# An edge-gated graph layer on one core: edge sums for two tiles at a time, additions in place, one more place for fetched rows

## The chip, the cores and the metric

The kernel runs on one core of a Trainium2 chip. The metric is the device time of the program in microseconds, as the median of several runs. The kernel before takes 1149.22 us (three runs, 1148.77 to 1149.63). The profile is of one execution, recorded by the hardware profiler.

## The reference: a gated sum over neighbours

The input `x` has 16 batches of 1024 nodes with 256 features, the adjacency matrix `adj` is 1024x1024 and mostly zero (one entry in about 128, and the diagonal). Cut to what matters:

```python
pre_u = jnp.einsum('bud,dk->buk', h_t, W1[:d])
pre_v = jnp.einsum('bvd,dk->bvk', h_t, W1[d:])
hidden = jax.nn.relu(pre_u[:, :, None, :] + pre_v[:, None, :, :] + b1)
S = jax.nn.sigmoid(jnp.einsum('buvk,ko->buvo', hidden, W2)[..., 0] + b2[0])
a_t = jnp.einsum('buv,bud->bvd', S * A_a, h_t)
m_t = jnp.einsum('uv,bud->bvd', A_m, h_t) * h_t
z_t = beta1 * h_t + beta2 * (jnp.einsum('bvd,de->bve', a_t, Wa) + ba) + beta3 * (jnp.einsum('bvd,de->bve', m_t, Wm) + bm)
```

Both adjacency arguments are `adj`. For each pair of a source u and a target v that `adj` connects, and for each batch, a gate is computed from a row of 256 sums. The features of u then go into two sums at v: one weighted by the entry of `adj`, one by entry times gate. Two 256x256 products, biases and the input itself make the output.

## The kernel before

**Tiling.** Only the connected pairs are computed. Targets come in 8 blocks of 128 (`vt`), batches in 4 groups of 4 (`g`, `GB` = 4). A pair of group and target block is a block `k`, 32 in all, in the list `order`. The edges of a target block are put into slots: two windows of 64 targets, five tiles of 128 edge slots each, so that a block has ten tiles and the whole program 320 (`n` counts them, `s` is the tile within its block). `lists` works out, for each target block, which source each slot holds and its entry of `adj`. It is a generator, cut into pieces that are laid between other work: four lists are made ahead of the first tile, four in the course of the first 120 tiles.

**The table.** For each group a table in DRAM has one row of 8 KB per source: the 4x256 values of `pre_u` and the 4x256 features. `rows` (L434) computes the first half of it with products on PE (L427), a copy on ACT (L443) and a DMA write on SP (L446); `copy_h` copies the second half from the input. `halves` (L452) computes `pre_v` + b1 for the targets of the next block, as two parts that add up exactly, `X`; its subtraction on DVE is L463.

**A tile.** These functions make one tile:
- `fetch` (L493): an indirect DMA, issued by POOL, brings the 128 rows of a tile into one of `NF` = 6 places `fetched` (L496). Tile n uses place n modulo 6.
- `expand` (L564): two products on PE (L569) spread `pre_v` of the targets over the edge slots, into the PSUM tile `pc`, of which there are two.
- `left_adj` (L573): ACT writes the adjacency weights of the slots, once for each of the four batches, into `left` (L579).
- `gate` (L598): DVE adds `fetched` and `pc` into the single buffer `t` (L601, 128x1024). Four operations then take the relu times W2 and its sum, a batch each (L606, 128x256). ACT turns the four sums into gates (L609) and multiplies the weights by them (L612, four operations). Pieces of a list go between the L606 (`fill`).
- `aggregate` (L614): PE sums over the slots (L623): for each batch a product with 32 columns of weights, 16 targets by two kinds. The four batches lie side by side in the array. A tile has one or two such rows of four products, by the quarters of the window that its slots can belong to; each fp32 product shows as two instructions in the trace.

**The end of a block.** `half_end` (L628) copies finished sums from PSUM (L631, ACT), `turn_over` (L633) transposes them on PE (L641), copies them into `LT` (L644, ACT) and multiplies the plain sums by the features of the target (L654, DVE). `block_end` (L659) forms the products with Wa and Wm on top of the bias (L672), two batches at a time; ACT copies them to `z` (L675), DVE adds beta1 times the input (L676), and SP stores the result (L678). The input rows `h_blk` are loaded by SP (L775). All small products share two PSUM banks (`small`). The last block has an end of its own, `tail`.

**Order.** The order of instructions on each engine is that of the program, written out by hand as one loop over n (L745). A step n issues, in this order: the edge sums of tile n-1 and the fetch of the tile that takes its place; the gate of tile n; the adjacency weights of n+1; what is due (`do`, work put off by `after` to a later step); the products `expand` of n+2; and then the small products, by the value of s: transposes at s = 1, 7 and 9, block end at 3 to 6, `halves` at 0, 2, 3, 5 and 6. Rows of the table come at steps written out as numbers (`plan`, L732 to L737), of which the second pair, for groups 2 and 3, matters here: up to one per block at s = 8 and one at s = 1.

## Time and profile before

| | |
|---|---|
| median of three runs | 1149.22 us |
| span of the profiled execution, first to last instruction | 1165.8 us |
| time of the profiled execution apart from its span | the page gives none |
| mean granted TensorE clock | 0.976 (0.94 from 71 to 300 us, then 1.00) |
| PE, DVE, ACT, POOL busy | 94%, 91%, 77%, 38% of the span |
| additions L601 | 320, the first at 71.6 us, the last at 1145.4 us |
| fetched rows (POOL's DMA queue) | 300.5 of 391.4 MB |

The profiled span is 16.6 us above the median of the runs; sums are made against it and then scaled. Busy times are sums of the lengths of instructions, without overlap. PE is shown busy while a matmul is in its pipeline, so a full row of PE can still have room; PEld is its weight load. "Idle before, releaser" is the time that an engine stood before an instruction, and what ended it. A loop step takes (1145.4 - 71.6)/319 = 3.37 us on the mean.

### The profile page before, as it was taken

The page shows a single profiled execution, that of the slowest core. Times are in us where ns is not written, and L with a number is a line of the kernel's source. Part 1 is how long each engine was busy: PE and PEld are TensorE (multiplying, and loading weights), DVE is VectorE, ACT ScalarE, POOL GpSimd, SP SyncE. Part 2 cuts the span into 40 slices and gives each one's busy share as a digit, 9 for nine tenths or more (in the row PEclk, how much of TensorE's full clock was granted, in tenths as well). Part 3 has the DMA queues.
Part 4 walks back from the last instruction along what each step waited for, and adds up shares of the span by engine and source line. Part 5 has one row for each costly group of instructions (what it writes and reads, how often), then busy time and mean ns, then how long its engine had stood idle before and what let it go on. Part 6 is the DMA issues. An engine that isn't in the chain of part 4 may idle for free. (4 is left out here: it accounts for less than half of the span.)

```text
span 1165.8 us, 23918 instructions
## 1 busy us (share of the span) xinstructions
PE 1092.1 (94%) x7633; PEld 723.1 (62%) x7633; DVE 1056.2 (91%) x3487; ACT 893.5 (77%) x2624; POOL 439.9 (38%) x428
## 2 busy tenths in 40 slices
PE   7867899999999999999999999999999999999986
PEld 6744666666666666666666666666666666666553
DVE  7688889888999989999999999999999999999994
ACT  2346587767887878888888888888888888888873
POOL 1556645253335333443333333333333333333330
PEclk9868899999999999999999999999999999999999
DMA  9986898999999999999999999999998998999991
GB/s 286 298 307 223 277 372 312 362 320 331 342 320 323 396 379 336 358 350 402 389 374 369 355 364 356 360 364 383 371 375 324 361 322 333 334 339 328 328 346 60
DMA packets 147048, 391.40 MB, mean 336 GB/s; under 512 B 16753, under 2 KB 105329, under 8 KB 110705
## 3 DMA queue, kind: packets, MB, share of 16 engines
q0 software_dynamic: 50016, 300.50, 68.9%
q1 hardware_dynamic: 81616, 74.99, 20.0%
q10 hardware_dynamic: 15280, 14.29, 3.7%
q8 instruction: 63, 1.03, 0.3%
q14 instruction: 73, 0.59, 0.1%
HBM read 393.78 MB, written 50.33 MB: 381 GB/s over the span
## 5 line engine op out<-in xcount | busy, mean ns | idle before, releaser
L496 POOL DMA_INDIRECT fetched<-table,uidx x320 | 341.5, 1067 | 628.3 <-PE acc L623 447.2
L606 DVE SCALAR_TENSOR_TENSOR t<-t,w_b 128x256 f32<-128x256 f32 x1280 | 478.3, 421 | 19.3 <-ACT left L612 0.5
L601 DVE TENSOR_TENSOR t<-fetched,pc 128x1024 f32<-128x1024 f32 x320 | 389.3, 1217 | 41.4 <-PE pc L569 13.9
L623 PE MATMUL acc<-fetched,left 128*32 128x256 f32 x4096 | 336.2, 391 | 31.9 <-ACT left L612 26.2
L612 ACT ACTIVATE left<-left,gt 128x32 f32<-128x32 f32 (+1 forms) x1280 | 299.3, 304 | 10.4
L569 PE MATMUL pc<-X,mark 128*128 128x512 f32 x640 | 237.6, 453 | 6.2 <-ACT mark L562 5.0
L623 PEld LDWEIGHTS acc<-fetched,left 128*32 128x32 f32 x4096 | 130.6, 109 | 179.3 <-issue 52.4
L569 PEld LDWEIGHTS pc<-X,mark 128*128 128x128 f32 x640 | 97.2, 191 | 140.0 <-issue 89.3
L609 ACT ACTIVATE gt<-sc,b_b 128x4 f32<-128x4 f32 x320 | 96.2, 301 | 43.4 <-DVE t L606 40.8
L672 PE MATMUL misc<-w_m,LT 128*128 128x256 f32 x496 | 117.2, 379 | 0.0
L672 PE MATMUL misc<-w_a,LT 128*128 128x256 f32 x496 | 117.1, 379 | 0.0
L579 ACT ACTIVATE left<-onehot,val 128x128 f32<-128x128 bf16 (+1 forms) x320 | 116.5, 364 | 0.0
L427 PE MATMUL misc<-w_v,hT 128*128 128x256 f32 x448 | 107.3, 383 | 0.0
L427 PE MATMUL misc<-w_u,hT 128*128 128x256 f32 x416 | 101.2, 390 | 5.7 <-ACT few L329 3.6
L606 DVE DVE_READ_ACCUMULATOR t<-t,w_b 128x1 f32 x1280 | 104.0, 81 | 0.0
L672 PEld LDWEIGHTS misc<-w_a,LT 128*128 128x128 f32 x496 | 93.9, 189 | 15.1
L672 PEld LDWEIGHTS misc<-w_m,LT 128*128 128x128 f32 x496 | 93.8, 189 | 14.9
L382 POOL DMA_INDIRECT val<-in_adjT_dram,vidx x80 | 85.7, 1071 | 35.1 <-issue 22.4
L427 PEld LDWEIGHTS misc<-w_v,hT 128*128 128x128 f32 x448 | 86.0, 192 | 13.9
L427 PEld LDWEIGHTS misc<-w_u,hT 128*128 128x128 f32 x416 | 79.5, 195 | 17.3 <-ACT few L329 3.7
L631 ACT COPY ev<-acc 128x512 f32<-128x512 f32 x128 | 75.5, 590 | 14.6 <-PE acc L623 4.2
L675 ACT COPY z<-misc 128x512 f32<-128x512 f32 x62 | 36.3, 586 | 58.1 <-PE misc L672 38.8
(164 smaller groups left out, 947.9 us busy)
## 6 DMA issues: line engine op xcount, KB each, us to landing
h_blk<-in_x_dram SPq DMA_DIRECT2D x31, 512.0 KB
out_dram<-z SPq DMA_DIRECT2D x31, 512.0 KB
hT<-in_xT_dram SPq DMA_DIRECT2D x28, 512.0 KB
table<-in_x_dram ACTq DMA_DIRECT2D x24, 512.0 KB
table<-tab SPq DMA_DIRECT2D x24, 512.0 KB
fetched<-table,uidx POOLq DMA_INDIRECT x320
table<-in_x_dram SPq DMA_DIRECT2D x8, 512.0 KB
table<-fetched SPq DMA_DIRECT2D x8, 512.0 KB
```

What stands on the lines that cost most here:

```text
L382: nc.gpsimd.indirect_dma_start(out=val[:, i, j:j + 1], out_offset=None, in_=adj_flat, in_offset=bass.IndirectOffsetOnAxis(ap=vidx[:, i, j: ...
L427: nc.tensor.matmul(p[:, bb * D:(bb + 1) * D], hT[:, 2 * h + bb, i, :], wt[:, i, :], start=(i == 0 and not begun), stop=(i == DC - 1), skip ...
L496: nc.gpsimd.indirect_dma_start(out=fetched[n % NF], out_offset=None, in_=table[g], in_offset=bass.IndirectOffsetOnAxis(ap=uidx[:, vt * NW ...
L569: nc.tensor.matmul(pcs[n][:, c], marks[n // TW][:, j * P:(j + 1) * P], cuts[k][:, w, c], start=True, stop=True)
L579: nc.scalar.activation(lefts[n][:, :m, :, 0, :], onehot[:, i, o:o + m, :].unsqueeze(2).to_broadcast([P, m, GB, V]), AF.Copy, scale=val[:, ...
L601: nc.vector.tensor_tensor(t, fetched[n % NF][:, :GD].rearrange("p (b d) -> p b d", b=GB), pcs.pop(n).rearrange("p (b d) -> p b d", b=GB), ...
L606: nc.vector.scalar_tensor_tensor(t[:, b, :], t[:, b, :], 0.0, w2_b, ALU.max, ALU.mult, accum_out=sc[:, b:b + 1])
L609: nc.scalar.activation(gt, sc, AF.Sigmoid, bias=b2_b)
L612: nc.scalar.activation(lefts[n][:, :m, b, 1, :], lefts[n][:, :m, b, 0, :], AF.Copy, scale=gt[:, b:b + 1])
L623: nc.tensor.matmul(accs[h][b * 2 * V:(b + 1) * 2 * V, r, :], left[:, i, b].rearrange("p k v -> p (k v)"), f[:, GD + b * D:GD + (b + 1) * D ...
L631: nc.scalar.copy(evs[q], accs.pop(q))
L672: nc.tensor.matmul(pz[:, bb * D:(bb + 1) * D], LTs[k][:, c, 2 * h + bb, i, :], wt[:, c, :], start=False, stop=(i == 0 and c == DC - 1), sk ...
```

## The change

Seven things change.
- The addition is a function of its own, `add`. It writes into the place of the fetched rows, and step n adds tile n+1 ahead of the gate of n. The gate works in place on the fetched rows; `t` is gone.
- Every second step (odd n) issues the edge sums of two tiles, n-3 and n-2, back to back, and then the two fetches that take their places; in the last three steps the sums follow at once.
- A place is taken from a list of free ones. There are 7, and after step 110 an eighth, in the memory of a new pool `lst`, which holds all buffers of the lists and is closed there.
- `left` has the adjacency weights twice instead of four times: its seven columns of 16 are laid out so that neighbouring batches share one. `LT` gets another order of its parts to match.
- `block_end` has no `z` and no copy on ACT: DVE reads the products from PSUM, adds and writes into `h_blk`, which is stored from there.
- The small products are moved: block end from s = 3 to 6 to s = 4 to 7, the transposes to s = 0, 2 and 8. Up to n = 120 they and `expand` stand ahead of addition and gate in the step, later behind.
- The last planned load of `plan` and its two row products come two steps earlier.

```diff
+    lst = ExitStack()
+    lists_done = lst.close
+    lst = lst.enter_context(tc.tile_pool(name="lst", bufs=1))
...
-    NF = 6
+    NF = 7
+    at_slot, free = {}, list(range(NF))
...
-        R = wk.tile([P, RC], FP, name="R", bufs=4)
+        R = lst.tile([P, RC], FP, name="R", bufs=4)
...
+        at_slot[n] = free.pop(0)
         nc.gpsimd.indirect_dma_start(
-            out=fetched[n % NF], out_offset=None, in_=table[g],
+            out=fetched[at_slot[n]], out_offset=None, in_=table[g],
...
-        lefts[n] = wk.tile([P, 2, GB, 2, V], FP, name="left")
-        nc.scalar.activation(lefts[n][:, :m, :, 0, :], onehot[:, i, o:o + m, :].unsqueeze(2).to_broadcast([P, m, GB, V]),
+        lefts[n] = wk.tile([P, 2, 2 * GB - 1, V], FP, name="left", bufs=5)
+        nc.scalar.activation(lefts[n][:, :m, 1::GB, :],
+                             onehot[:, i, o:o + m, :].unsqueeze(2).to_broadcast([P, m, GB // 2, V]),
                              AF.Copy, scale=val[:, i, j:j + 1])
...
+    def add(n):
+        t = fetched[at_slot[n]][:, :GD]
+        nc.vector.tensor_tensor(t, t, pcs.pop(n), ALU.add)
+
     def gate(n):
-        k, g, vt, w, j = where(n)
-        t = one.tile([P, GB, D], FP, name="t")
-        nc.vector.tensor_tensor(t, fetched[n % NF][:, :GD].rearrange("p (b d) -> p b d", b=GB),
-                                pcs.pop(n).rearrange("p (b d) -> p b d", b=GB), ALU.add)
+        m = len(QUARTERS[n % TW])
+        t = fetched[at_slot[n]][:, :GD].rearrange("p (b d) -> p b d", b=GB)
...
-            nc.scalar.activation(lefts[n][:, :m, b, 1, :], lefts[n][:, :m, b, 0, :], AF.Copy, scale=gt[:, b:b + 1])
+            nc.scalar.activation(lefts[n][:, :m, 2 * b, :], lefts[n][:, :m, 1 + b // 2 * GB, :],
+                                 AF.Copy, scale=gt[:, b:b + 1])
...
-                                 left[:, i, b].rearrange("p k v -> p (k v)"), f[:, GD + b * D:GD + (b + 1) * D],
+                                 left[:, i, 2 * b - b % 2:2 * b - b % 2 + 2].rearrange("p k v -> p (k v)"), f[:, GD + b * D:GD + (b + 1) * D],
...
-            LTs[k] = one.tile([P, DC, GB, 2, P], FP, name="LT")
+            LTs[k] = one.tile([P, GB, 2, DC, P], FP, name="LT")
...
-        after(step + (1 if k == BS - 1 else 2), times_h)
+        after(step + (1 if k == BS - 1 or w else 2), times_h)
...
-            nc.scalar.copy(z[:, sl], pz.rearrange("p (b d) -> p b d", b=2))
-            after(step + 2, lambda sl=sl: nc.vector.scalar_tensor_tensor(z[:, sl], hb[:, sl], be1, z[:, sl],
-                                                                         ALU.mult, ALU.add))
-        after(step + 3, lambda: nc.sync.dma_start(
-            out[g * GB:(g + 1) * GB, vt * P:(vt + 1) * P, :].rearrange("b p d -> p b d"), z))
+            after(step + 1, lambda sl=sl, pz=pz: nc.vector.scalar_tensor_tensor(
+                hb[:, sl], hb[:, sl], be1, pz.rearrange("p (b d) -> p b d", b=2), ALU.mult, ALU.add))
+        after(step + 2, lambda: nc.sync.dma_start(
+            out[g * GB:(g + 1) * GB, vt * P:(vt + 1) * P, :].rearrange("b p d -> p b d"), hb))
...
-                                                                             for i in range(2, NT - 1)), (223, 231, 233)))
+                                                                             for i in range(2, NT - 1)), (221, 229, 231)))
...
-        if 1 <= n <= total:
-            aggregate(n - 1)
-            fetch_val(2)
-            if n - 1 + NF < total:
-                fetch(n - 1 + NF)
-            if n % TW in (0, MID + 1):
-                half_end(n - 1, 0 if n % TW else 1)
+    def products(n, k, s):
+        nonlocal end, parts, piece, last
+        if (s == 2 and 0 < k < BS) or n == total:
             turn_over(k - 1, 1, 1, n)
-        if s in (3, 4, 5, 6) and 0 < k < BS:
-            if s == 3:
+        if s in (4, 5, 6, 7) and 0 < k < BS:
+            if s == 4:
                 end = block_end(k - 1)
                 next(end)
             go(end, n)
-        if s == 7 and k < BS:
+        if s == (8 if n < total - T else 7) and k < BS:
             turn_over(k, 0, 0, n)
             turn_over(k, 0, 1, n)
-        if s == 9 and k < BS:
-            turn_over(k, 1, 0, n)
+        if (s == 0 and 0 < k < BS) or n == total - 1:
+            turn_over(k - (s == 0), 1, 0, n)
...
+    add(0)
+    def refill():
+        nonlocal ahead
+        while free and ahead < total:
+            fetch(ahead)
+            ahead += 1
+    def gather_in(n):
+        aggregate(n)
+        free.append(at_slot.pop(n))
+        fetch_val(2)
+        refill()
+        if (n + 1) % TW in (0, MID + 1):
+            half_end(n, 0 if (n + 1) % TW else 1)
+    for n in range(total + 2):
+        k, s = divmod(n, T)
+        if n < total - 3:
+            last_in = n - 1 if n % 2 else done
+        else:
+            last_in = n
+        while done < min(last_in, total):
+            gather_in(done)
+            done += 1
...
+        if n < 120:
+            if n + 2 < total:
+                expand(n + 2)
+            products(n, k, s)
+        if n + 1 < total:
+            add(n + 1)
         if n < total:
             gate(n)
             if n + 1 < total:
                 left_adj(n + 1)
...
+        if n >= 120 and n + 2 < total:
+            expand(n + 2)
...
         fill(n, False)
+        if n >= 120:
+            products(n, k, s)
+        if n == ROOM:
+            lists_done()
+            more = main.enter_context(tc.tile_pool(name="more", bufs=1))
+            for i in range(MORE):
+                free.append(len(fetched))
+                fetched.append(more.tile([P, 2 * GD], FP, name=f"fetched{len(fetched)}"))
+            refill()
```

## The prediction

> **What bounds the kernel now.** I read the shares by engine first, then the stages, then single steps. PE is busy 94% and DVE 91% of the span, so the shares leave both open. The stages are in the table of busy time by stretch (columns: stretch, length, then busy time and count of each engine, TensorE clock, DMA share, GB/s); the two 10 us rows are from a finer one:

> ```profile
> 71.00:300.00 229.00, 208.46 (x1354) 138.50 (x1353) 196.47 (x670) 161.07 (x469) 114.34 (x112) 0.94 0.89 311
> 300.00:500.00 200.00, 194.40 (x1393) 128.50 (x1392) 190.71 (x646) 162.16 (x480) 81.92 (x77) 1.00 0.96 353
> 500.00:900.00 400.00, 395.96 (x2859) 260.83 (x2860) 378.13 (x1190) 338.71 (x1009) 138.88 (x129) 1.00 0.99 366
> 900.00:1146.70 246.70, 236.26 (x1704) 149.56 (x1704) 236.50 (x745) 203.63 (x619) 78.98 (x76) 1.00 0.90 327
> ```

> The same table for the line of the additions (L601) counts 58, 59, 125 and 79 tiles in them. A block is ten tiles, so a block takes 39.5, 33.9, 32.0 and 31.2 us. To see what a block is made of I went to the timeline of DVE (start, length) in a late block:

> ```profile
> 1107.41 0.74 DVE L676 SCALAR_TENSOR_TENSOR z<-h_blk,be,z 128x512 f32<-128x512 f32 x1
> 1108.08 1.21 DVE L601 TENSOR_TENSOR t<-fetched,pc 128x1024 f32<-128x1024 f32 x1
> 1109.32 0.42 DVE L606 SCALAR_TENSOR_TENSOR t<-t,w_b 128x256 f32<-128x256 f32 x1
> ...
> 1110.36 0.42 DVE L606 SCALAR_TENSOR_TENSOR t<-t,w_b 128x256 f32<-128x256 f32 x1
> ...
> 1110.88 1.22 DVE L601 TENSOR_TENSOR t<-fetched,pc 128x1024 f32<-128x1024 f32 x1
> 1112.21 0.43 DVE L606 SCALAR_TENSOR_TENSOR t<-t,w_b 128x256 f32<-128x256 f32 x1
> ```

> From start to start: L606 to the next L606 0.347; the last L606 to L601 0.52; L601 to L606 1.33, or 1.24 when another operation came before L601. With three 0.347 per tile and the five extra operations of a block (two L676 at 0.67, two L654 at 0.61, one L463 at 1.14), a block sums to 5x1.33 + 5x1.24 + 30x0.347 + 5x0.52 + 5x0.347 + 3.70 = 31.3 us. The measured period from one L676 (981.89) to the same one of the next block (1013.18) is 31.29. So DVE alone sets the late pace: from 900 on it waits 1.1 us in total. PE is "busy" because matmuls overlap in its records, and waits there for ACT. In 500 to 900 DVE's waits are 8.8 us, and DMA stands at a share of 0.99, with a ceiling near 1.03 where it is fullest (530 to 570: 1.02 to 1.05).

> PE pays at each change between the edge sums (32 columns) and full matmuls. Weight loads in the timeline of PE:

> ```profile
> 603.54 0.59 PEld L623 LDWEIGHTS acc<-fetched,left 128*32 128x32 f32 x16 [0.33 <-ACT mark L562]
> 604.54 0.30 PEld L569 LDWEIGHTS pc<-X,mark 128*128 128x128 f32 x2 [0.41 <-issue]
> ```

> Both loads stand idle at the change, 0.33 and 0.41, each tile. In matmul starts: 1.82 from eight L672 to L623 instead of 8x0.213 (0.11 lost), 1.00 for 16 L623 instead of four groups of 0.215 (0.14), 0.57 for two L569 instead of 0.43 (0.14): 0.39 us a tile.

> [...] independent operations start before the end of the one before (0.347 apart at a length of 0.42), and one that waits for its own engine starts 0.17 later. [...] L713 reads PSUM at 128x512 in 0.75, L676 SBUF in 0.75. [...] No row shows a landing.

> **The change, part by part.**

> *Additions in place, a tile ahead.* L601 no longer writes the single buffer t, so it stops waiting for the L606 just before it, and the first L606 finds its sum a tile old. In the built program the addition has lost its wait on DVE. Without a wait, a 128x1024 addition is followed after 1.14 (L463 at 1006.52, L601 at 1007.66), and an L606 after 0.347. Saved a block: 5x(1.33-1.14) + 5x(1.24-1.14) + 5x(0.52-0.347) = 2.3 us; new sum 29.0. From below: 0, if the gaps are fixed; from above 2.3. I take 2.3, since the list of waits of the built program shows the cause gone. It is work on the bounding engine.

> *Edge sums of two tiles together.* 160 pairs of changes fewer, 62 us of PE. PE isn't the bound, so this is worth nothing by itself: it is hidden behind DVE, and without that cover would be up to 1.9 us a block. Late, PE's own work (128 L623 in groups of four 6.9, 20 L569 4.3, 48 of L672 and L427 10.2, their 4 bias rows 0.9, 16 L641 1.7, changes 3.9) is 27.9, then 25.9. The sums move one to two tiles later, with them their fetches on POOL and the copies of acc on ACT: PE no longer meets a gate of the tile just done, which removes most of 26.2 us of PE waiting for L612.

> *Slots.* A row place is now held from the addition until the second of two sums. Before: a fetch issued at 614.41 served the addition at 628.98, a lead of 14.6. With seven places the sums of a pair can start when ACT has weighted the second tile, some 2 us into a DVE step (L609 0.30, L612 0.96, waits); with 1 us for the first sum and 1.07 for the issue (L496) its fetch is under way after about 4.5, and is wanted four steps after the start of that one: at 3.0 to 3.4 us a step 7.5 to 9 us ahead. The second has a step more, less its own 1 us of issue. From tile 110 on, an eighth place adds a step. [...] Upper: if landing takes the whole old lead, some 5 us for each of 55 pairs. The queue moves a fetch's share (77% of bytes) in about 3.0 us at 405 GB/s, so two ahead and itself make 9: just in time. I take a third of the gain before tile 110 as lost.

> *Output straight from PSUM.* 62 copies L675 (0.586 each, 0.48 start to start: 30 us) leave ACT, whose 58 us of waiting before them goes too; L683 then takes DVE as long as L676. New wait: the second product's bank is free only after L683 at the end of DVE's step 8. In the built program the second group of transposes of step 8 waits for it from tile 120 on. Behind it on PE stand, where there is a table row product (tiles 128, 138, 158, 188 to 228: 8 blocks), 8x0.213, then the edge sums of step 9 and the two L569 products of the tile that DVE adds at the start of step 10: 0.43 + 1.71 + 0.11 + 1.72 + 0.14 + 0.57 + some 0.2 of pipeline = 4.9 against a DVE step of 1.14 + 4x0.347 = 2.53. DVE loses 2.3 us in such a block, and 0.6 in one without the row product. PE then has nothing else to run in front.

> *The rest.* L579 writes half as much: by its two forms (386 ns at 128, 332 at 64) 54 ns less x192 and an estimated 27 x128, 14 us of ACT, hidden, as ACT is at 85%. The load of h_blk waits for the store to land, since both use one buffer: on SP the hT load and table write stand behind; two 0.52 MB transfers against six steps (18 us) until L683, hidden; uncovered, some 3 us a block. Moved transposes, pool renaming and the changed layout of LT keep counts and sizes: 0. The last tiles are summed at once, so the end is unchanged, and one more initial fetch costs POOL 1 us ahead of work that waits for lists: 0.

> **Sum against the profiled span.** Late, 7.9 blocks: (2.3-0.6)x7.9 = 13.4. 500 to 900, 12.5 blocks: DVE gives 2.3 less the mean wait (8x2.3 + 4.5x0.6)/12.5 = 1.7, so 0.6; DMA's floor 32.0x0.99/1.03 = 30.8 allows 1.2; the new wait will overlap some of the old 0.7, so I take 0.9: 11. 300 to 500: two thirds of 2.3, 5.9 blocks: 9. The first 229 us, where PE and DVE both fall short of full: the same 1.5, 5.8 blocks: 9. Together 42: span 1165.8 to 1124. The median of the runs is 1149.2, 0.986 of the span, and the page gives the execution no other time; scaled, 1149.2 - 42 = 1107.

> **The rivals.**
> *More of it arrives.* The new bank wait is absorbed, because PE, freed of changes and of ACT, runs further ahead. For: 25.9 of PE work in 29. Against: DMA's floor, 1.2 to 1.8 a block at a ceiling of 1.03 to 1.05. Late 2.3x7.9 = 18, middle 1.45x12.5 = 18, earlier 12 and 12: 1149 - 60 = 1089.
> *The gaps stay.* If 1.33 and 0.52 don't come from the own wait, or the bank wait costs every block 2.3, only the early relief of PE and ACT is left, some 6 us: 1143. Against: the 1.14.
> *Fetches late, slower.* With seven places, DVE waits at the addition for the first fetch of a pair. 42 us over 55 pairs is 0.76, so it decides when landings overrun the lead by 0.76 us on the mean, that is, take longer than about 9 us; at an overrun of 1 us it is 55 less 42, so 1162. For: share 0.96 and 0.99, two issued together. Against: the DVE waited only 2.8 us for fetches before, and the stages before tile 110 are the slowest, which lengthens the lead.
> *It comes out even,* where these meet.

> **How the numbers follow.** Forecast (1095 to 1126) 0.58, more of it 0.13, gaps stay 0.14, even 0.04, slower 0.11. Within 0.2%, 2.3 us, a measurement can't tell it from no change. Faster 0.85, same 0.04, slower 0.11. The range leaves out the slower tenth and the best half of the second case: 1084 to 1145; the forecast's own is 1095 to 1126.

> **What would show it.** L606 after the addition starts at 1.14, and the addition at 0.35 after L606; a late block at 29.0 to 29.8 between L683s; idle time before the weight loads of the edge sums once in two tiles; PE waiting for DVE's L683 at the transposes of step 8, and DVE right after for the products. Wrong, if DVE's waits name fetches by more than 30 us, or if the period late stays above 31.

## The result: slower, 1194 us instead of 1107

The changed kernel takes 1194.41 us (median of four runs, 1191.46 to 1196.33), the kernel before 1149.11 beside it: a ratio of 1.0392, 95% interval 1.0363 to 1.0421. The forecast was 1107 with a range of 1084 to 1145. The profiled execution took 1195.8 us with a span of 1193.9.

The table of busy time by stretch of the changed kernel, cut where tiles 0, 60, 120, 240 and 319 are added (columns: stretch, length, busy time and count of PE, PEld, DVE, ACT and POOL, TensorE clock, DMA share, GB/s):

```profile
71.80:298.70 226.90, 199.09 (x1380) 137.68 (x1383) 197.58 (x698) 158.20 (x474) 115.45 (x111) 0.94 0.92 325
298.70:515.30 216.60, 193.47 (x1413) 134.42 (x1405) 189.35 (x650) 156.50 (x479) 88.16 (x82) 0.95 0.92 331
515.30:926.90 411.60, 373.47 (x2764) 261.43 (x2764) 348.17 (x1143) 305.96 (x946) 124.92 (x121) 0.97 0.94 347
926.90:1168.30 241.40, 218.44 (x1713) 147.00 (x1714) 227.02 (x749) 188.78 (x601) 84.17 (x76) 0.96 0.92 334
```

In the kernel before, the same stretches took 237.8, 203.8, 384.4 and 247.8 us. By these two traces 10.9 us are won up to tile 60 and 6.4 from tile 240 on, and 12.8 and 27.2 are lost between. They must be read with care: the profiled execution of the kernel before has a span 16.6 us above the median of its runs here, so the two spans are 28 us apart and the medians 45. Some 17 us of the loss are in no comparison with this trace; the second group shows where to look for them. DVE is no longer full in the middle: 348 of 412 us, and the clock, which was 1.00 from 300 us on, is 0.95 to 0.97.

The gain that the prediction counted on is in the timeline of DVE (start, length), in a late block:

```profile
1104.31 1.21 DVE L606 TENSOR_TENSOR fetched<-fetched,pc 128x1024 f32<-128x1024 f32 x1
1105.44 0.42 DVE L614 SCALAR_TENSOR_TENSOR fetched<-fetched,w_b 128x256 f32<-128x256 f32 x1
...
1106.47 0.42 DVE L614 SCALAR_TENSOR_TENSOR fetched<-fetched,w_b 128x256 f32<-128x256 f32 x1
1106.82 1.22 DVE L606 TENSOR_TENSOR fetched<-fetched,pc 128x1024 f32<-128x1024 f32 x1
```

Addition to gate is 1.13 instead of 1.33, gate to addition 0.35 instead of 0.52. What took it back is in the list of waits (engine, line, waited for: us in total, times, longest). DVE and PE in the changed kernel:

```profile
DVE fetched L606 <- PE pc L574: 112.0, 51, 6.3
DVE fetched L606 <- DMA fetched<-table,uidx: 22.3, 20, 3.5
...
PE misc L649 <- DVE h_blk L683: 40.6, 20, 2.3
```

and the same line of DVE in the kernel before:

```profile
DVE t L601 <- PE pc L569: 13.9, 18, 2.0
```

From tile 120's addition to the end the sum of the two traces closes: DVE waits 78 us for products and rows where it waited 7 (the additions' two main lines, both traces cut at that tile), less 20 blocks at 2.3 us that its operations give back (46), is 25 more; measured are 678.6 less 652.6, 26. So the question is why the addition now waits for L574. The prediction had one reason at hand, the bank of L683, and it is there, exactly 20 times. In the timelines of PE and DVE of a block with a row product:

```profile
788.93 0.63 PE L649 MATMUL misc<-ident,ev 128*128 128x128 f32 x4 [1.90 <-DVE h_blk L683]
790.18 3.41 PE L431 MATMUL misc<-w_u,hT 128*128 128x256 f32 x8 [0.62 <-ACT LT L652]
793.52 1.93 PE L631 MATMUL acc<-fetched,left 128*32 128x256 f32 x32
795.38 1.19 PE L574 MATMUL pc<-X,mark 128*128 128x512 f32 x4
```

```profile
796.15 1.22 DVE L606 TENSOR_TENSOR fetched<-fetched,pc 128x1024 f32<-128x1024 f32 x1 [4.85 <-PE pc L574]
```

The chain is the one described (transposes, row product, two tiles' sums, products, addition), but DVE loses 4.85 us, not 2.3: the row product takes 3.41 us where eight such products took 1.89 in the kernel before, and the trace has TensorE at half clock from 789.7 to 793.1 us. Adding up the stretches that the trace records at half clock gives 126.5 us, 82.1 of it after 230 us; in the kernel before 57.5 and 6.3.

### The profile page after: what moved, and what is told of

The parts are those of the page before. It is cut to its first block, busy times and chain, and to the rows that moved or that the text cites. A ratio compares the mean times of both kernels' runs of the same rounds, so it can differ in the third digit from the quotient of the medians.

```text
span 1193.9 us, 23757 instructions
## 1 busy us (share of the span) xinstructions
PE 1047.5 (88%) x7633; PEld 730.3 (61%) x7633; DVE 1020.6 (85%) x3487; ACT 841.7 (70%) x2562; POOL 439.3 (37%) x428
## 3 DMA queue, kind: packets, MB, share of 16 engines
q8 instruction: 62, 1.02, 0.3%
## 4 chain that ended last, share of the span: by engine, by line
DVE 36%; PE 31%; issue 12%; ACT 10%; DMA 8%; POOL 1%; ACTq 0%; DVEq 0%; POOLq 0%
DVE fetched L614 17%; PE misc L431 10%; DVE fetched L606 10%; PE acc L631 10%; DMA fetched<-table,uidx 7%; PE pc L574 4%; ACT left L619 3%; PE misc L680 3%; PE misc L649 2%; DVE h_blk L683 2%; ACT LT L652 2%; DVE low L467 2%; ACT gt L617 1%; PE misc L435 1%; DVE LT L663 1%
## 5 line engine op out<-in xcount | busy, mean ns | idle before, releaser
L606 DVE TENSOR_TENSOR fetched<-fetched,pc 128x1024 f32<-128x1024 f32 x320 | 388.4, 1214 | 135.7 <-PE pc L574 112.0
L614 DVE SCALAR_TENSOR_TENSOR fetched<-fetched,w_b 128x256 f32<-128x256 f32 x1280 | 474.5, 417 | 0.0
L631 PE MATMUL acc<-fetched,left 128*32 128x256 f32 x4096 | 272.7, 400 | 2.6 <-ACT left L619 2.6
L574 PE MATMUL pc<-X,mark 128*128 128x512 f32 x640 | 222.9, 448 | 15.7 <-DVE fetched L606 7.3
L574 PEld LDWEIGHTS pc<-X,mark 128*128 128x128 f32 x640 | 107.3, 190 | 98.8 <-issue 44.4
L649 PE MATMUL misc<-ident,ev 128*128 128x128 f32 x512 | 83.2, 287 | 67.4 <-DVE h_blk L683 40.6
L431 PE MATMUL misc<-w_u,hT 128*128 128x256 f32 x416 | 117.4, 435 | 15.9 <-ACT LT L652 8.8
L649 PEld LDWEIGHTS misc<-ident,ev 128*128 128x128 f32 x512 | 62.2, 145 | 92.4 <-ACT gt L617 43.7
L584 ACT ACTIVATE left<-onehot,val 128x64 f32<-128x64 bf16 (+1 forms) x320 | 102.8, 321 | 0.0
L614 DVE DVE_READ_ACCUMULATOR fetched<-fetched,w_b 128x1 f32 x1280 | 102.1, 80 | 0.0
```

The lines of the kernel that those rows point to most:

```text
L431: nc.tensor.matmul(p[:, bb * D:(bb + 1) * D], hT[:, 2 * h + bb, i, :], wt[:, i, :], start=(i == 0 and not begun), stop=(i == DC - 1), skip ...
L574: nc.tensor.matmul(pcs[n][:, c], marks[n // TW][:, j * P:(j + 1) * P], cuts[k][:, w, c], start=True, stop=True)
L584: nc.scalar.activation(lefts[n][:, :m, 1::GB, :], onehot[:, i, o:o + m, :].unsqueeze(2).to_broadcast([P, m, GB // 2, V]), AF.Copy, scale=v ...
L606: nc.vector.tensor_tensor(t, t, pcs.pop(n), ALU.add)
L614: nc.vector.scalar_tensor_tensor(t[:, b, :], t[:, b, :], 0.0, w2_b, ALU.max, ALU.mult, accum_out=sc[:, b:b + 1])
L631: nc.tensor.matmul(accs[h][b * 2 * V:(b + 1) * 2 * V, r, :], left[:, i, 2 * b - b % 2:2 * b - b % 2 + 2].rearrange("p k v -> p (k v)"), f[ ...
```

## The experiments

Two theories to begin with. **Bank:** the wait for L683's bank is the cause, only dearer than thought. **Clock:** PE, with less to do and in bursts of two tiles, leaves stretches idle and is then halved. A third came up after the second group. The runs fell on chips on which the kernel before takes 1149 (the changed kernel, the second and fifth group) or 1169 to 1173 us (the other groups), so each ratio is to the kernel before in the same group; the changed kernel as it is ran on the first kind alone. The one trace of the kernel before has a span as on the second kind (1165.8 us, where the runs there have 1162 to 1177 and those on the first kind 1142 to 1155), though its chip is not known. "From tile 120" is from that tile's addition to the end of the profiled execution.

**First group: without the bank wait, and with more work on PE.** The first issues what is due (`do`, L683 among it) between addition and gate:

```diff
+        if n >= 120:
+            do(n)
         if n < total:
             gate(n)
...
-        do(n)
+        if n < 120:
+            do(n)
```

> From tile 120 on, the work that is due is done between the addition and the gate of a step, so DVE frees the bank of the second product about 1.4 us sooner in step 8; nothing else moves. Theory A (PE stands for that bank in step 8, 20 times 2.0 us, its clock is halved after such a stand, and DVE then waits for the products of expand): the stand falls from 1.9 to about 0.5 us, the halved stretches after tile 120 mostly go, DVE's wait for expand after tile 120 falls from 78 us to under 35, time about 1150 (1140 to 1165). Theory B (the two sums together, or seven places, make PE and the fetches late, the bank is a bystander): within 10 us of 1194.

The second moves the second transposes and the row product to step 9 (the planned load of the last block goes two steps back with it):

```diff
-            turn_over(k, 0, 1, n)
+            if not 120 <= n < total - T:
+                turn_over(k, 0, 1, n)
+        if s == 9 and 120 <= n < total - T:
+            turn_over(k, 0, 1, n)
...
-            at.update((n, k) for n in pieces)
+            at.update((n + (n >= 120 and n % T == 8), k) for n in pieces)
```

> From tile 120 on, the second group of transposes and the row product of step 8 go to step 9, behind the edge sums and the expand products; the last planned row products are back at 231 and 233. PE then meets the bank a step later, when it is long free. Theory A: no wait of PE for L683 left, block period 29 to 31 us after tile 120, time 1135 to 1155. Theory B: within 10 us of 1194.

The third has ACT copy the output from its bank to a used part of LT at once, and DVE read it there:

```diff
+            z = LTs[k][:, 2 * h].rearrange("p k c n -> p (k c n)")
+            nc.scalar.copy(z, pz)
```

> One part undone: ACT copies the output product out of PSUM again (into a used part of LT), which frees the bank at once, and DVE adds from SBUF. Theory A: no wait of PE for L683, though ACT gets 62 copies (30 us) back and stands for PE before them; time 1140 to 1165. Theory B: no change, or slower by up to 10 us through ACT.

The fourth leaves the wait and gives PE two useless products ahead of the first transposes of step 8:

```diff
+        if w == 0 and q == 0 and 120 <= step < total - T:
+            for i in range(WARM):
+                nc.tensor.matmul(pt.rearrange("p r k c v -> p (r k c v)"), w_a[:, 0, :P], w_a.rearrange("p c k -> p (c k)"), start=True, stop=True)
```

> As the changed kernel, with two extra 128x512 products (about 1.7 us of PE, their output is overwritten) ahead of the first transposes of step 8 from tile 120 to 310: PE works where it stood, the bank comes no sooner. This tells the wait itself from the halved clock. If the halved clock after the stand does much of the harm: the halved stretches after tile 120 go and the time falls by 15 to 30 us, to 1165 to 1180. If the wait alone does it: 1190 to 1215, as the extra products cost nothing while PE waits and something where it doesn't.

| edit | ratio (95%) | from tile 120 | at half clock |
|---|---|---|---|
| L683 sooner | 1.0622 (1.0544 to 1.07) | 684.6 | 125.8 |
| transposes apart | 1.055 (1.0456 to 1.0644) | 672.8 | 137.0 |
| copy by ACT | 1.0636 (1.0541 to 1.0731) | 681.9 | 160.9 |
| two useless products | 1.0309 (1.0256 to 1.0362) | 661.9 | 92.1 |

None of the three without the bank wait is clearly better than the changed kernel: 672.8 from tile 120 at best, where two profiles of that kernel, on the faster chips, have 678.6 and 672.0. The waits of DVE from tile 120 on when the transposes are apart:

```profile
DVE fetched L606 <- PE pc L574: 42.5, 20, 9.1
DVE fetched L606 <- PE acc L631: 17.0, 14, 1.8
```

The bank theory falls. The wait for L683 is nearly gone (0.9 us with the transposes apart, 6.0 with L683 sooner, 40.6 in the changed kernel), and the additions still wait for PE, by the two lines 59.5 us where the changed kernel has 78 and 71; what is saved there comes back as other waits of DVE, and the stretch is as long as it was. With L683 sooner, DVE waits 29.9 us at L663 for ACT instead. The clock theory gains: the run with useless work is the best of the four, and from tile 120 on no block has a stretch at half clock (clock 1.00 from 979.1 to 1038.7 us, two late blocks, where the changed kernel has 0.97 from 956.6 to 1017.7). But it is still slower than the kernel before, and from tile 120 on its DVE waits 40.8 us for products and 18.6 more by the line of the edge sums.

**Second group: one part alone, one part undone.** The changed kernel again; the kernel before with nothing but the addition in place and a tile ahead; the changed kernel with sums of one tile a step; the changed kernel with the addition back at its own gate.

> The changed kernel unaltered, next to the three below on one chip. If the early blocks (tiles 10 to 120) were 30 us longer in the first four experiments because of their edits, this run shows its old start, tile 120 at 515 us, and about 1194. If they were longer because of the chip, tile 120 starts near 545 here too, and the kernel before is again some 20 us above its 1149.

```diff
+    def add(n):
+        t = fetched[n % NF][:, :GD]
+        nc.vector.tensor_tensor(t, t, pcs.pop(n), ALU.add)
...
+        if n + 1 < total:
+            add(n + 1)
         if n < total:
             gate(n)
```

> The kernel before with one part of the change alone: additions in place, a tile ahead. Edge sums stay single, the output still goes through a copy, six places. Clock theory (what hurts is that TensorE gets idle lumps and is then halved for 3.4 us): TensorE keeps its 27.9 us of work in small groups, hardly any stretch at half clock after 250 us, late block 29 to 30, 20 to 40 us below the kernel before on the same chip. Rival, the addition ahead is itself what hurts (a place is held a step longer, the fetch has a step less): VectorE waits for fetched rows by more than 30 us and the time is that of before or above.

```diff
-            last_in = n - 1 if n % 2 else done
+            last_in = n - 1
```

> The changed kernel with the pairing alone undone: the edge sums of one tile in every step, all else as changed. Clock theory: time at half clock falls from 126 us to 60 to 80, since the bursts and lumps of two tiles are gone; 25 to 45 us below the changed kernel on the same chip, with TensorE's wait for L683 in step 8 still there. Rival, the bank wait or the order from tile 120 on is the cause whatever the sums do: within 10 us of the changed kernel. Rival, TensorE becomes the bound with its 62 us back: late block above 31.

```diff
-        if n + 1 < total:
-            add(n + 1)
         if n < total:
+            add(n)
             gate(n)
```

> The changed kernel with the addition put back to the step that uses it (still in place), pairing and the rest as changed. VectorE's late step is long again, 31.3 a block. Clock theory: TensorE, with less work and a longer step, is idle more and is halved at least as often as in the changed kernel, 110 us or more, and the time is equal to the changed kernel's or up to 25 us above. Rival, the addition ahead is what hurts: the time comes back to within 10 us of the kernel before.

| kernel | ratio (95%) | DVE's wait for products | lead, tiles 120 to 239 / 240 to 309 |
|---|---|---|---|
| before | 1 | 13.9 | 1.1 / 2.7 |
| changed, again | 1.0463 (1.0418 to 1.0507) | 111.2 | 1.5 / 1.9 |
| before, addition ahead | 1.022 (1.0175 to 1.0265) | 84.8 | 0.25 / 0.14 |
| changed, single sums | 1.0337 (1.0295 to 1.0379) | 102.3 | 1.0 / 1.9 |
| changed, addition at the gate | 1.0041 (1.0018 to 1.0064) | 4.7 | 2.8 / 3.6 |

The lead, worked out from the traces, is the mean time from the end of a tile's products (L574, L569) to the start of its addition. DVE in the kernel before with the addition ahead, and in the changed kernel with the addition at the gate:

```profile
DVE fetched L600 <- PE pc L569: 84.8, 109, 7.6
```

```profile
DVE fetched L606 <- PE pc L574: 4.7, 4, 2.0
```

The changed kernel again adds tile 120 at 514.6 us, as at first, while the first group did so at 543.8 to 558.5. I put those 30 us down to the chip, since three of those four edits act from tile 120 on only; the changed kernel itself was not run on that chip, so this is argued. The rest is the turn of the study. Putting the addition back takes away nearly the whole loss, with pairs, output from PSUM and seven places kept; putting the addition ahead into the kernel before makes it slower by itself. Undoing the pairs brings 8 us, not the 25 to 45 that the clock theory wanted. The clock is not the origin either: with the addition at the gate PE has as little to do, in the same pairs, and is at half clock for 67.6 us, where that theory expected 110 or more. The third theory, **lead:** the addition reads `pc`, which PE makes. The change moved the addition a step earlier and left `expand(n + 2)` in the step where it was. In the kernel before, a whole step of PE's work lay between these products and the step that reads them; now the next step reads them at its start. What PE had in hand evened out its unequal steps, and that is used up. The mean lead alone does not tell how far: in tiles 120 to 239 it is longer in the changed kernel than in the one before (1.5 and 1.1), and yet from tile 120 on DVE waits 78 us for products in the one and 4.6 in the other.

The profiles of these runs, on one chip, also show where the time went. With the addition at the gate tile 120 is added at 494.1 us instead of 514.6, and the rest takes 655.0 instead of 672.0: more than half of what is won back lies ahead of tile 120. DVE up to there, in the changed kernel again and with the addition at the gate:

```profile
DVE fetched L606 <- PE pc L574: 39.9, 20, 5.2
```

```profile
DVE fetched L606 <- PE pc L574: 2.6, 2, 2.0
```

If the kernel before takes the 652.6 us from tile 120 on of its profile on this chip too, its median, less the 2 us by which times are longer than spans, leaves some 495 for the start of that tile: an estimate, by which the changed kernel loses about 20 us before tile 120, and not the 2 that the two traces at the head have between them.

**Third group: how early is too early?** The addition of tile n+1 goes between the four products of tile n, ahead of the last or of the second. An operation still stands between addition and reader.

```diff
         for b in range(GB):
+            if b == 3 and n + 1 < total:
+                add(n + 1)
             fill(n)
```

> The changed kernel with the next tile's addition put ahead of the last of the four products of the tile before, not of the first. VectorE's sum is that of the changed kernel (one product stands between the addition and the first product that reads it, so neither waits for the operation just before it), late block 29.0 to 29.8; but the addition is 0.35 us early and not 1.4. Lead theory (an early addition eats the time by which TensorE's products for a tile are ready before VectorE adds them, 3.6 us late and 2.8 in the middle with the addition at the gate, 1.9 and 1.5 ahead of all four): leads near 3.2 and 2.3, VectorE's wait for the products under 35 us, 1115 to 1150. Rival, any addition ahead of the gate puts VectorE into the loop of gate, weights, sums and products, wherever it stands: 1180 or more. Rival, the clock: a shorter VectorE step makes the TensorE idle more, 100 us or more at half clock, whatever the place.

With `b == 1`:

> As the run before, with the addition ahead of the second of the four products, 1.04 us early. Lead theory: between the changed kernel and the run before it, VectorE's wait for the products 60 to 100 us, 1155 to 1185. Rival, all that matters is whether an operation stands between the addition and its reader: equal to the run before within 5 us.

With `b == 3` and the transposes apart, as in the first group:

> The addition ahead of the last product, and the second transposes of step 8 with the row product moved to step 9 from tile 120 on, so that no product waits for the output's bank. If the bank wait costs what the prediction put on it once the lead is back, 2.3 us in eight blocks and 0.6 in the others, this is 15 to 25 us below the run without the move. Rival, it is hidden by the lead or moved to another wait: within 8 us of it.

With `b == 3` in the kernel before, sums single, output copied, six places:

> The kernel before, with the addition in place and ahead of the last of the four products; sums single, copy of the output and six places as before. Lead theory: the lead of before (2.7 late, 1.1 in the middle) loses 0.35 and what VectorE gains; late block no longer than 30.5, in the middle, where the lead was small, no gain: 1130 to 1150. Rival, single sums leave TensorE no room at all (60.8 of 62.6 us busy late in the kernel before), so that nothing is gained without the pairing: 1149 or more.

| kernel | ratio (95%) | DVE's wait for products | late block |
|---|---|---|---|
| changed, ahead of the last | 1.0261 (1.0189 to 1.0333) | 60.7 | 30.4 |
| changed, ahead of the second | 1.0325 (1.0281 to 1.037) | 71.8 | 31.0 |
| changed, ahead of the last, transposes apart | 1.0206 (1.015 to 1.0262) | 62.9 | 28.8 or 30 |
| before, ahead of the last | 0.9924 (0.9894 to 0.9953) | 47.8 | 30.5 |

The list puts more waits of the addition down to PE's edge sums: 29.1 and 34.2 us in the first two rows, under 5 in the others. From tile 120 on, with these added, the additions wait 2.1 us at the gate, 43.4, 63.9, and 71.3 ahead of all four. So the order is as the lead theory wants it; the sizes are not: ahead of the last was to be under 35 us in all and no slower than before, and is 2.6% slower. Its leads are 2.7 late and 1.5 in the middle, not 3.2 and 2.3. With the transposes apart the interval overlaps the run without the move, so the bank wait is at most a minor term. The last row is the only run here that is faster than the kernel before, 1159.34 against 1169.04, about as much as was expected of it. Its lead is used up nearly as far as with the addition ahead of all four (0.3 us, in the middle and late), but the waits are 47.8 us and not 84.8.

**Fourth group: give the lead back.** The addition stays ahead of all four products; `expand` moves with it.

```diff
         if n + 1 < total:
             add(n + 1)
...
-            if n + 2 < total:
-                expand(n + 2)
+            if n + 3 < total:
+                expand(n + 3)
```

> The changed kernel, addition ahead of all four products as it is, with one thing moved after it: TensorE's products for a tile are issued right after the addition that frees their bank, a step earlier than in the changed kernel (tile n+3 and not n+2 in step n). Lead theory: the lead late is back at 3 us or more and about 2.5 in the middle, VectorE's wait for the products falls from 111 us below 40, time 1110 to 1150, whatever chip takes 1149 for the kernel before (20 more where it takes 1169). Rival, the loop of gate, weights, sums and products or the clock sets the pace: within 10 us of the changed kernel, with VectorE's wait still above 80.

The same with the transposes apart; the kernel before with the addition ahead and `expand(n + 3)`; and the first with the two useless products:

> The same with the second transposes of step 8 and the row product moved to step 9 from tile 120 on, so that TensorE does not wait for the output's bank. If the bank wait costs 2.3 us in eight blocks and 0.6 in the others once the lead is there, 15 to 25 us below the run without it; if it is hidden by the lead or turns into another wait, within 8.

> The kernel before with the addition in place and ahead of all four products (1.022 of the kernel before as it was), now with the products for a tile issued a step earlier too. Lead theory: late block 29 to 30.3, VectorE's wait for the products below 40 (85 without it), 0.975 to 0.995 of the kernel before. Rival, TensorE with single sums is full: late block 31.3 again and 1.01 to 1.03.

> The lead back as in the first run, with two extra 128x512 products ahead of the first transposes of step 8 from tile 120 on, so that fewer stretches fall to half clock. If the half clock costs by itself even with a lead, 5 to 15 us below the first run; if the lead covers it, equal or up to 8 above.

| kernel | ratio (95%) | wait for products | for fetched rows | at half clock |
|---|---|---|---|---|
| changed, lead back | 1.033 (1.0261 to 1.0399) | 16.5 | 59.4 | 135.6 |
| and transposes apart | 1.0689 (1.0652 to 1.0726) | 9.8 | 56.7 | 162.9 |
| before, addition ahead, lead back | 0.999 (0.9963 to 1.0016) | 13.5 | 54.0 | 51.8 |
| changed, lead back, useless products | 1.0426 (1.0395 to 1.0457) | 21.7 | 52.9 | 109.2 |

DVE in the changed kernel with the lead back:

```profile
DVE fetched L606 <- DMA fetched<-table,uidx: 59.4, 34, 4.1
...
DVE fetched L606 <- PE pc L574: 16.5, 16, 3.0
...
DVE h_blk L683 <- DMA h_blk<-in_x_dram: 10.2, 1, 10.2
```

and in the kernel before with the addition ahead and the lead back:

```profile
DVE fetched L600 <- DMA fetched<-table,uidx: 54.0, 49, 3.7
DVE fetched L600 <- PE pc L569: 13.5, 12, 2.0
DVE fetched L600 <- PE misc L643: 11.4, 7, 2.5
DVE fetched L600 <- PE acc L625: 7.7, 6, 4.2
```

As a cause of the wait, the lead is shown: in both kernels, with no other edit, the wait for products falls from 111 to 16.5 and from 84.8 to 13.5. With all that the additions wait for PE it is from 113 to 21 and from 88 to 36. In the kernel before with the addition ahead the time comes with it, 1.022 to 0.999, though not to the expected 0.975 to 0.995. In the changed kernel it mostly does not (1.039 to 1.046 before, 1.033 now), and the expected 1110 to 1150 was wrong. With the wait for PE mostly gone, DVE meets the next ones. With the transposes apart it is slower still, against both expectations; there DVE waits 32.3 us for the load of `h_blk` and 30.4 for ACT. Useless products cut the half clock by 26 us and bring no gain (1.0426 against 1.033), so with a lead the half clock costs nothing that these runs show. Late blocks alternate between 28.8, close to the prediction's 29.0, and 38 to 40; the timelines of DVE and of SP in a long one:

```profile
1031.13 0.75 DVE L683 SCALAR_TENSOR_TENSOR h_blk<-h_blk,be,misc 128x512 f32<-128x512 f32 x1 [10.19 <-DMA h_blk<-in_x_dram]
```

```profile
1014.55 0.37 SPq L852 DMA_DIRECT2D h_blk<-in_x_dram  x1
```

The load is issued at 1014.55 and its reader goes 16.6 us later. Input and output of a block share this one buffer, so the load waits for the store of the block before: late, it is issued 0.5 us after that store in the kernel before, about 5.8 in the changed one, and up to 18 here. Why the store takes so much longer here is not shown.

**Fifth group: a second buffer, and the early tiles.** First, on top of the lead back, a second `h_blk` for every other block from tile 130 on, in the memory that the lists leave:

```diff
+            odd = n > 120 and k % 2
+            hbs[k - 1] = more.tile([P, GB, D], FP, name="h_odd") if odd else big.tile([P, GB, D], FP, name="h_blk", bufs=1)
```

> The changed kernel with the products a step earlier, as in the run with the lead back, and from tile 130 on a second buffer for h_blk in every other block, so that the load of a block's old rows no longer waits for the store of the block before. With the lead back, late blocks alternated between 28.8 and 38 to 40, and in the long ones VectorE waited up to 10.2 us at L683 for that load. Theory of the chain of slack (lead first, then the shared buffer): late blocks 28.8 to 30 without exception, VectorE's wait for the load gone from 10.2 to under 3 in all, from tile 120 to the end 666 before, 625 to 645 now; what is lost before tile 120 (38 us to the kernel before on such a chip) stays, so 1.000 to 1.020 of the kernel before. Rival, TensorE's half clock makes the long blocks by itself: they stay at 36 to 40, and the ratio at 1.03.

Then, on top, single sums and the addition ahead of the last product, with `expand(n + 2)`, up to tile 120:

```diff
+        if n < 120:
+            last_in = n - 1
...
+            if b == 3 and n < 120:
+                add(n + 1)
```

> The same from tile 120 on; before it, sums of one tile in every step and the addition ahead of the last of the four products, as in the kernel that took 0.992 of the kernel before. If what is lost before tile 120 comes from the pairs and the early addition while fetches, lists and TensorE are all short of slack, tile 120 begins within 10 us of the kernel before, and the whole is 0.97 to 0.995 of it. Rival, the loss lies in what both keep (products a step later in the block, seven places, the shared buffer): tile 120 begins 25 us or more late again.

| kernel | ratio (95%) | start of tile 120 | tiles 120 to 249 | 250 to 309 |
|---|---|---|---|---|
| two h_blk | 1.0361 (1.0304 to 1.0418) | 533.8 | 428.2 | 176.4 |
| and early tiles as said | 1.0108 (1.0064 to 1.0152) | 513.2 | 419.1 | 175.7 |
| before, its profile | 1 | 513.2 | 416.2 | 188.1 |

Before tile 120, DVE's wait for fetched rows in the first of these two, and in the second (the same list, cut to that stretch):

```profile
DVE fetched L606 <- DMA fetched<-table,uidx: 53.6, 40, 4.3
```

```profile
DVE fetched L606 <- DMA fetched<-table,uidx: 0.8, 1, 0.8
```

The long late blocks are gone, so the shared buffer made them and not the clock (granted clock 0.955 on the mean, 0.945 in the run before, which was on another chip): 28.8 to 31.1 each, 11.7 us less than in the trace of the kernel before over six blocks. Early, pairs, early additions and early products together cost 20.6 us, and DVE's 53.6 us of waits for rows go with them. Most of it is the products a step earlier, for the changed kernel without them, on other chips of this kind, added tile 120 at 515.3 and 514.6. So the lead given back cost some 19 us ahead of tile 120, and with the second buffer it brought 13 to 20 from there on (659.0 us instead of 672.0 and 678.6). Both runs miss their expected ratios: tiles 120 to 249 take 428 and 419 us and not less than the 416 of before. The equal 513.2 in the table are no equal start either: the second run has 648.6 from tile 120 on, 4 less than the trace of before, and is 1.1% slower, so by the estimate above some 15 us are still lost early. Waits for products (up to 8.1 us at once), rows and ACT's copies share that stretch, and which of them would have to go first was not tried.

## Why the prediction was wrong, by its steps

- **The addition ahead, "from below: 0 ... I take 2.3"**: the step that failed. DVE's operations do give 2.3 us a block, but the lower bound was no bound. The step priced the waits that the addition drops, and not the one that comes nearer: its other operand is made by PE, whose products were not moved. Alone it makes the kernel before 2.2% slower (a gain of 42 us was forecast for the whole), and DVE's wait for products grows from 13.9 to 84.8 us. Late in the kernel before, 2.7 us of lead covered PE's unequal steps; the prediction read that DVE hardly waits (1.1 us from 900 on, 8.8 from 500 to 900), and did not ask what kept this small.
- **Pairs, "worth nothing by itself"**: about right. With the addition at the gate the whole rest of the change is 1.004; with it ahead, undoing the pairs brings 8 us. "PE then has nothing else to run in front" was seen, but only for step 8.
- **The bank of L683, 2.3 us in eight blocks and 0.6 in others**: mechanism and count right (20 waits, 40.6 us), but not what decides. Runs without it were no better; with the transposes apart 59.5 us of the additions' waits for PE stayed from tile 120 on. Its price in the block shown, with a row product, was half of what the trace has (4.85); the row product alone took 3.41 us at half clock instead of 1.89, and the half clock was not in the sum at all. That PE had become the slack engine was worked out (25.9 in 29); that it would then be at half clock for 126.5 us instead of 57.5 was not.
- **Seven places, a third of the gain before tile 110**: an estimate, for no view shows how long a fetch takes to land, and too small once PE is no longer in the way. In the changed kernel DVE waits 22.3 us for rows, all before tile 120; with the lead back and two h_blk, 53.6 there. The rival "fetches late" was right as a second layer, not as the cause.
- **300 to 500 and the first 229 us, 9 us won in each**: the other way, by the estimate of the second group: some 20 us lost ahead of tile 120. Putting the addition back gains 20.5 there.
- **Load and store of h_blk, "hidden; uncovered, some 3 us a block"**: hidden in the changed kernel, as said. Uncovered it cost 10.2 us in the block shown: the reader went 16.6 us after the load's issue, which itself came 16.2 after the store's.
- **Late block 29.0 to 29.8**: 29.7 in blocks without half clock, 31.3 with a stretch of it; 28.8 where all covers hold. Of the prediction's own two signs of being wrong, the late period above 31 came true in every other block, the 30 us of waits for fetches did not (22.3).
- **Rivals:** the slower one had 0.11 and the wrong mechanism. Missing was the rival "the addition waits for PE" at every block and not only behind the bank.

## What to carry to other kernels

When a read is moved earlier, list everything that it reads and move each producer by as much, or price the lead that is given up: the time between the end of the producer and the read in the trace, which no list of waits shows as long as it is positive. Read it tile by tile, for its mean can hide tiles that have none. Then ask what is covered next: here products, fetched rows and a shared buffer each hid behind the one before, and mending one brought out the next. A small step at the right place (the addition one operation early, not four) was worth more than the large one: 0.992 of the kernel before. And before two traces are set against each other, compare their spans with the medians: a difference between them is a part of the gap that the traces can't place.
